# Two float32r products with exactly split activations, and query-major attention, in a two-layer hybrid block

## The chip, the core and the metric

The kernel runs on one core of a Trainium2 chip. The metric is the device time of one execution in microseconds. TensorE multiplies matrices into PSUM, VectorE and ScalarE do arithmetic and copies, GpSimd a little, SyncE issues transfers.

## The reference

The input is 8 images of 32 x 32 positions with 384 channels, all in float32. A first layer adds to each image a windowless attention with 6 heads of 64 over all 1024 positions; a second layer adds a causal attention with one head of 384 and, on the first five images, a feed-forward part whose weights are only signs:

```python
# layer 0
qkv = group_norm(x) @ qkv_w + qkv_b
attn = (q * SCALE) @ k.T + rel_h[..., None] + rel_w[..., None, :]   # per head, 1024 x 1024
x = x + softmax(attn) @ v @ proj_w + proj_b
# layer 1
t = t + softmax(causal(q @ k.T * 384**-0.5)) @ v                    # q, k, v of layer_norm(t)
h = quantize(layer_norm(t) @ sign(W1 - mean).T + b1)                # 384 -> 1536
t = t + quantize(gelu(h) @ sign(W2 - mean).T + b2)                  # 1536 -> 384
```

`quantize` scales by the largest absolute value over the whole image and clips. With 8 images and five groups, one image is a group; images 5 to 7 keep zeros here, so nothing is added to them.

## The kernel before, in words

Images follow one another. `run` loads an image as 8 tiles of 128 positions (`xt`), passes it through `layer0`, `attention1` and, for the first five, `ffn`, and stores it. A scheduler orders the instructions of each engine's queue by the data and the buffers that they need, so that pieces of neighbouring stages are mixed; within an engine they run in that order. Buffers come from pools with a fixed number of them: PSUM has two score tiles of two banks (`s_tile`) and four single banks (`o_tile`).

- `group_norm_T` (L222) reads the image a second time, already transposed by the host (`img_T`), takes statistics on VectorE, joins channels to groups and back with small matmuls (L238, L246), and scales in place (L264).
- `layer0` (L341) makes q and k (`project_T`, L295) and v (`project`, L305), and adds the relative positions as 64 further rows of q and k: small products (L379, L380), copied out by VectorE (L383) and then by ScalarE (L386).
- `attend0_fast` (L392) is key-major. For a pair of heads and a tile of 128 keys `scores` puts keys on partitions and all 1024 queries along the free dimension (L400), ScalarE takes the exp without a maximum (L404), VectorE adds the tiles of probabilities up (L412), and L416 multiplies them with v, 64 columns of weights for each head, so that two heads share the array. The probabilities are never transposed. `divide` (L421) gets the denominators by a product with ones (L428), transposes, inverts and multiplies them in. The output product (L463) follows for the 8 tiles.
- `attend1_fast` (L520) does the same for the causal attention (L531, mask L536, exp L539, values L545); a column of ones in v yields the denominator.
- `check` and `judge` gather sums and reciprocals; if one is out of bounds, a second copy of the whole program with the maximum subtracted (`attend0_general`, `attend1_general`) runs after the first. On the given inputs it does not run.
- `layer_norm_T` (L269) normalizes a tile (L284), transposes it by TensorE (L219) and copies it out (L220).
- `ffn` (L607): 12 tiles of 128 features with `w1b` (L295), bias (L614), absolute maximum (L615); after the last one the scale; then clamp (L618) and gelu (L619) over each feature tile with all 1024 positions; then for each of 8 token tiles 12 products with `w2b` (L625), bias and maximum (L626, L627), quantization and sum (L630, L631). All products are float32.
- `binarize` (L188) makes the signs at the start, in the layout of `z - (z - sign)`, five passes over a weight.

Of the kernel before, what the change touches and what calls it, by code (L numbers as in the profile page):

```python
# [9 lines left out]
F32 = mybir.dt.float32  # L10
I32 = mybir.dt.int32
# [23 lines left out]
SUM_MAX, RSUM_MAX = 1e28, 1e22  # L35


class Pools:
    def __init__(self, ctx, tc, path):
        self.path, self.fast = path, path == "f"  # L40

        def pool(name, bufs, **kw):
            return ctx.enter_context(tc.tile_pool(name=f"{path}_{name}", bufs=bufs, **kw))

        self.x = pool("x", 1)
        self.wide_ = pool("wide", 2)
        self.big_ = pool("big", 2)
        self.v_ = pool("v", 1)
        self.page_ = pool("page", 10 if self.fast else 8)
        self.work = pool("work", 2)  # L50
        self.small = pool("small", 4)
        self.ps_s = pool("ps_s", 2, space=PSUM)
        self.ps_o = pool("ps_o", 4, space=PSUM)

    def s_tile(self, name):
        return self.ps_s.tile([P, 2, 512], F32, tag="s", name=f"{self.path}_{name}")

    def o_tile(self, name):
        return self.ps_o.tile([P, 512], F32, tag="o", name=f"{self.path}_{name}")

    def big(self, name):
        return self.big_.tile([P, 2, 3, T], F32, tag="big", name=f"{self.path}_{name}")

    def wide(self, name, dtype=F32):
        return self.wide_.tile([P, NC, T], dtype, tag="wide", name=f"{self.path}_{name}")

    def page(self, name, dtype=F32):
        return self.page_.tile([P, T], dtype, tag="page", name=f"{self.path}_{name}")

    def v(self, name):  # L70
        return self.v_.tile([P, NJ, C + 1], F32, tag="v", name=f"{self.path}_{name}")


@with_exitstack
def conv_attn_hybrid(
# [3 lines left out]
    img_T: bass.AP,  # L79
# [17 lines left out]
    const = ctx.enter_context(tc.tile_pool(name="const", bufs=1))  # L97

    def load_x(pools, b):
        t = pools.x.tile([P, NJ, C], F32, tag="x", name=f"{pools.path}_x_{b}")
        src = x[b].rearrange("(j p) c -> p j c", p=P)
        for q in range(4):
            nc.sync.dma_start(out=t[:, 2 * q : 2 * q + 2, :], in_=src[:, 2 * q : 2 * q + 2, :])
        return t

# [10 lines left out]
    for half in range(2):  # L118
# [3 lines left out]
    w1b = load("w1b", [P, NC, FF], w1T.rearrange("(k p) o -> p k o", p=P), nc.scalar)  # L122
    w2b = load("w2b", [P, NM, C], w2T.rearrange("(k p) o -> p k o", p=P), nc.scalar)
# [11 lines left out]

    maskT = const.tile([P, P], F32, name="maskT")
    nc.gpsimd.memset(maskT, 0.0)
    nc.gpsimd.affine_select(
        out=maskT, in_=maskT, compare_op=ALU.is_ge, fill=MASKED, base=0, pattern=[[1, P]], channel_multiplier=-1
    )  # L140
# [30 lines left out]
    N_SEEN = B * (NPAIR + 1)  # L171
    seen = const.tile([P, 2, N_SEEN], F32, name="seen")
    flag = const.tile([1, 1], I32, name="flag")

    def judge(pools):

        bad = const.tile([P, 2, N_SEEN], F32, name="bad")
        for i, most in enumerate((SUM_MAX, RSUM_MAX)):
            nc.vector.tensor_scalar(bad[:, i, :], seen[:, i, :], most, -1.0, ALU.is_lt, ALU.mult)
        worst = const.tile([P, 1], F32, name="worst")  # L180
        nc.vector.tensor_reduce(worst, bad, AX.XY, ALU.max)
        nc.vector.tensor_scalar_add(worst, worst, 1.0)
        ps = pools.o_tile("bad")
        nc.tensor.matmul(ps[0:1, 0:1], worst, ones[:, 0:1], start=True, stop=True)
        nc.vector.tensor_copy(flag, ps[0:1, 0:1])


    def binarize(pools, w, nk, n_out, name):  # L188
        gs = n_out // NG
        n = NG * gs  # L190
        part = const.tile([P, NG], F32, name=f"part_{name}")
        for g in range(NG):
            nc.vector.tensor_reduce(part[:, g : g + 1], w[:, :, ts(g, gs)], AX.XY, ALU.add)
        tot = pools.o_tile(f"tot_{name}")
# [3 lines left out]
        z = pools.big(f"z_{name}").rearrange("p a b t -> p (a b t)")[:, : nk * n_out].rearrange("p (k o) -> p k o", k=nk)  # L198
        s = pools.big(f"s_{name}").rearrange("p a b t -> p (a b t)")[:, : nk * n_out].rearrange("p (k o) -> p k o", k=nk)
        for g in range(NG):  # L200
            nc.vector.tensor_scalar(z[:, :, ts(g, gs)], w[:, :, ts(g, gs)], mean[:, g : g + 1], None, ALU.subtract)
        z, s = z[:, :, :n], s[:, :, :n]
        nc.vector.tensor_scalar(s, z, 0.0, None, ALU.is_gt)

        nc.vector.scalar_tensor_tensor(s, z, 0.0, s, ALU.is_lt, ALU.subtract)
        nc.vector.tensor_tensor(s, s, z, ALU.add)
        nc.vector.tensor_tensor(w[:, :, :n], z, s, ALU.subtract)
        if n < n_out:
            nc.vector.memset(w[:, :, n:], 0.0)


    def stages(pools):

        def transpose_tiles(dst, srcs, engine):

            n = len(srcs)
            pt = pools.o_tile("pt")
            for i, s in enumerate(srcs):
                nc.tensor.transpose(pt[:, ts(i, P)], s, ident)  # L219
            engine(dst, pt[:, : n * P].rearrange("p (i q) -> p i q", i=n))  # L220

        def group_norm_T(b):  # L222

            xT = pools.wide(f"gnT_{b}")
            src = img_T[b].rearrange("(k p) t -> p k t", p=P)
            for k in range(NC):
                nc.sync.dma_start(out=xT[:, k, :], in_=src[:, k, :])
            st = pools.small.tile([P, NC, 2, 6], F32, tag="gst", name=f"gst_{b}")
            mv = pools.small.tile([P, NC, 2], F32, tag="gmv", name=f"gmv_{b}")
            for k in range(NC):  # L230
                for half in range(2):
                    nc.vector.bn_stats(st[:, k, half, :], xT[:, k, ts(half, 512)])
                nc.vector.bn_aggr(mv[:, k, :], st[:, k, :, :].rearrange("p a s -> p (a s)"))

            def over_groups(src, name):
                ps = pools.o_tile(name)
                for k in range(NC):
                    nc.tensor.matmul(  # L238
                        ps[:GROUPS_GN, 0:1], to_group[:, k, :], src(k), start=(k == 0), stop=(k == NC - 1)
                    )  # L240
                return ps[:GROUPS_GN, 0:1]

            def to_channels(src, n, name):
                ps = pools.o_tile(name)
                for k in range(NC):
                    nc.tensor.matmul(ps[:, k * n : (k + 1) * n], of_group[:, ts(k, P)], src, start=True, stop=True)  # L246
                return ps[:, : NC * n].rearrange("p (k n) -> p k n", k=NC)

            gm = pools.small.tile([GROUPS_GN, 2], F32, tag="gm", name=f"gm_{b}")
# [13 lines left out]
            for k in range(NC):  # L263
                nc.vector.tensor_scalar(  # L264
                    xT[:, k, :], xT[:, k, :], cs[:, k, 0:1], cs[:, k, 1:2], ALU.subtract, ALU.mult
                )
# [427 lines left out]
```

## Time and profile before

| | us |
|---|---|
| median of 3 runs | 3450.17 (3449.17 to 3451.05) |
| the profiled execution | 3451.05 |
| its span | 3449.1 |
| TensorE busy | 3191.1 |
| VectorE busy | 1345.3 |
| ScalarE busy | 851.4 |

A page of the profile gives, for each engine, the time in which it is busy; the chain of work that ended last, followed back from the end; and groups of instructions with count, busy time, mean duration in ns, and the idle time of the engine before them with what ended it. PE is TensorE's matmul, PEld its load of weights, DVE VectorE, ACT ScalarE, POOL GpSimd.[...] `f_` stands before the names of the path without a maximum.

### The profile page before, as it was taken

Reading aid. Unit: us, or ns where it says so; the run is one execution under the profiler, and the core shown is the slowest. Engines: PE = TensorE matmul, PEld = TensorE weight load, DVE = VectorE, ACT = ScalarE, POOL = GpSimd, SP = SyncE. Lnnn points to the kernel's source line nnn. Section 1 sums busy time; section 2 is a strip of 40 time slices with the busy share of each in tenths; the row PEclk is TensorE's granted clock in tenths of the full one; section 3 lists DMA queues with packets and bytes.
Section 4 is the critical chain, followed back from the end, with each engine's and each line's share of the span. In section 5 each row is a group of like instructions: output and inputs, shape, how many; then the busy total and the mean of one; then the engine's idle time right before and its main releaser. Section 6 shows DMA issues by size and latency. Waiting matters only on the chain.

```text
span 3449.1 us, 26310 instructions
## 1 busy us (share of the span) xinstructions
PE 3191.1 (93%) x10958; PEld 1525.6 (44%) x10958; DVE 1345.3 (39%) x2085; ACT 851.4 (25%) x935; POOL 163.8 (5%) x139
## 2 busy tenths in 40 slices
PE   0999998999989999989999889999899999999999
PEld 0534544435445345444354543454443454355344
DVE  7344333452233442334533344523335324523442
ACT  0332120431213321304311223213043114212320
POOL 1100002000010000020000010000200020002000
PEclk9999998999999999989999989999899999999999
DMA  4000001000000000010000010000100010000000
GB/s 147 1 0 0 0 19 37 1 0 1 0 23 32 1 0 0 19 37 1 0 0 0 19 37 0 1 0 19 37 1 0 19 37 1 0 28 28 1 0 20
DMA packets 28031, 49.03 MB, mean 14 GB/s; under 512 B 4224, under 2 KB 24064, under 8 KB 27904
## 3 DMA queue, kind: packets, MB, share of 16 engines
q1 hardware_dynamic: 20864, 37.75, 3.1%
q10 hardware_dynamic: 7040, 9.51, 0.8%
q8 instruction: 88, 1.44, 0.2%
q14 instruction: 39, 0.32, 0.0%
HBM read 34.68 MB, written 12.58 MB: 14 GB/s over the span
## 4 chain that ended last, share of the span: by engine, by line
PE 89%; DVE 6%; ACT 3%; DMA 1%; issue 0%; POOL 0%
PE f_s L400 20%; PE f_av L416 10%; PE f_y L625 9%; PE f_y L295 9%; PE f_qk L295 8%; PE f_v L305 7%; PE f_av L545 5%; PE f_s L531 5%; PE f_q L295 4%; PE f_k L295 4%; PE f_pj L305 3%; ACT f_qa L386 3%; PE f_pt L219 1%; PE f_den L428 1%; DVE f_x L631 1%; DVE f_y L630 1%
## 5 line engine op out<-in xcount | busy, mean ns | idle before, releaser
L400 PE MATMUL f_s<-f_qa,f_ka 128*128 128x512 f32 x1536 | 708.6, 607 | 8.5 <-ACT f_qa L386 8.5
L404 ACT ACTIVATE f_pr<-f_s 128x1024 f32<-128x1024 f32 x384 | 393.6, 1025 | 653.5 <-PE f_s L400 653.4
L412 DVE TENSOR_TENSOR f_sum<-f_sum,f_pr 128x1024 f32<-128x1024 f32 x288 | 351.4, 1225 | 370.2 <-ACT f_pr L404 370.2
L400 PEld LDWEIGHTS f_s<-f_qa,f_ka 128*128 128x128 f32 x1536 | 279.9, 191 | 431.0 <-issue 315.6
L416 PE MATMUL f_av<-f_pr,f_v 128*64 128x512 f32 x1536 | 366.7, 603 | 0.0
L625 PE MATMUL f_y<-w2b,f_h 128*128 128x384 f32 x960 | 325.7, 504 | 29.2 <-ACT f_h L619 29.2
L295 PE MATMUL f_y<-f_lnT,w1b 128*128 128x512 f32 x720 | 314.8, 597 | 2.8 <-ACT f_lnT L220 2.8
L295 PE MATMUL f_qk<-f_gnT,wqkv_sb 128*128 128x512 f32 x576 | 269.6, 632 | 9.5 <-DVE f_gnT L264 9.5
L625 PEld LDWEIGHTS f_y<-w2b,f_h 128*128 128x128 f32 x960 | 188.8, 197 | 167.1 <-ACT f_h L619 39.1
L295 PEld LDWEIGHTS f_y<-f_lnT,w1b 128*128 128x128 f32 x720 | 136.6, 192 | 169.4 <-issue 165.0
L416 PEld LDWEIGHTS f_av<-f_pr,f_v 128*64 128x64 f32 x1536 | 94.2, 136 | 253.6 <-issue 222.7
L545 PE MATMUL f_av<-f_v,f_pr 128*128 128x385 f32 x576 | 194.5, 486 | 0.0
L531 PE MATMUL f_s<-f_qk 128*128 128x512 f32 (+3 forms) x576 | 193.8, 486 | 0.0
L295 PEld LDWEIGHTS f_qk<-f_gnT,wqkv_sb 128*128 128x128 f32 x576 | 116.7, 204 | 156.5 <-issue 152.7
L615 DVE TENSOR_REDUCE am<-f_h 128x1 f32<-128x1024 f32 x60 | 73.2, 1220 | 248.4 <-ACT f_h L614 248.4
L545 PEld LDWEIGHTS f_av<-f_v,f_pr 128*128 128x128 f32 x576 | 108.6, 190 | 78.6 <-issue 11.5
L531 PEld LDWEIGHTS f_s<-f_qk 128*128 128x128 f32 x576 | 103.0, 190 | 83.0 <-issue 57.4
L305 PE MATMUL f_pj<-wproj_sb,f_oT 128*128 128x384 f32 x384 | 128.1, 490 | 9.6 <-DVE f_oT L439 9.6
L386 ACT COPY f_qa<-f_rel 32x384 f32<-32x384 f32 x128 | 103.0, 805 | 123.5 <-DVE f_qa L383 120.6
L354 POOL COPY f_ka<-ident 32x1024 f32<-32x1024 f32 x96 | 102.8, 1071 | 594.9 <-PE f_y L625 320.8
L295 PE MATMUL f_q<-f_lnT,wq_sb 128*128 128x512 f32 x288 | 130.3, 597 | 0.0
L295 PE MATMUL f_k<-f_lnT,wk_sb 128*128 128x512 f32 x288 | 128.8, 592 | 0.0
(125 smaller groups left out, 2519.2 us busy)
## 6 DMA issues: line engine op xcount, KB each, us to landing
f_x<-in_x SPq DMA_DIRECT2D x32, 384.0 KB, 5.1
f_gnT<-in_xT SPq DMA_DIRECT2D x24, 512.0 KB, 4.5
out_y<-f_x SPq DMA_DIRECT2D x32, 384.0 KB, 2.5
w1b<-in_w1T ACTq DMA_DIRECT2D x1, 2304.0 KB, 10.4
w2b<-in_w2T ACTq DMA_DIRECT2D x1, 2304.0 KB, 16.3
wqkv_sb<-in_qkv_w ACTq DMA_DIRECT2D x1, 1728.0 KB, 8.7
wproj_sb<-in_proj_w ACTq DMA_DIRECT2D x1, 576.0 KB, 4.5
wq_sb<-in_wq ACTq DMA_DIRECT2D x1, 576.0 KB, 17.3
```

Source lines behind the costliest of these rows:

```text
L295: nc.tensor.matmul(ps[:, half, :], w[:, k, cols], xT[:, k, ts(half, 512)], start=(k == 0), stop=(k == NC - 1),)
L305: nc.tensor.matmul(ps[:, :C], xT[:, k, ts(j, P)], w[:, k, cols], start=(k == 0), stop=(k == NC - 1))
L354: nc.gpsimd.tensor_copy(ka[r, par, p, :].rearrange("i (h w) -> i h w", h=H), unit)
L386: nc.scalar.copy(qa[rw, par, :, :].rearrange("k p (h w) -> k p w h", h=H)[:, :, 4 * g : 4 * g + 4, :], pv[rw])
L400: nc.tensor.matmul(sc[:, half, :], ka[:, par, p, ts(c, P)], qa[:, par, p, ts(half, 512)], start=True, stop=True)
L404: nc.scalar.activation(pr, sc.rearrange("p a n -> p (a n)"), AF.Exp)
L412: nc.vector.tensor_tensor(sums[par], prev, prs[par], ALU.add)
L416: nc.tensor.matmul(avs[half][ts(par, HD), :], v[:, c, ts(h, HD)], prs[par][:, ts(half, 512)], start=(c == 0), stop=(c == NJ - 1),)
L531: nc.tensor.matmul(sc[:, half, lo:], qk[:, 1, k, ts(c, P)], qk[:, 0, k, half * 512 + lo : (half + 1) * 512], start=(k == 0), stop=(k == NC ...
L545: nc.tensor.matmul(av[:, : C + 1], prs[c][:, ts(j - c, P)], v[:, c, :], start=(c == 0), stop=(c == j))
L615: nc.vector.tensor_reduce(am[:, m : m + 1], h[m], AX.X, ALU.max, apply_absolute_value=True)
L625: nc.tensor.matmul(ps[:, :C], h[m][:, ts(j, P)], w2b[:, m, :], start=(m == 0), stop=(m == NM - 1))
```

## The change

The whole attention code goes back to one form, query-major with a maximum, and the products with the sign weights change their type.

- Both attentions: scores have 128 queries on partitions and the keys along the free dimension. VectorE takes the row maximum (L303), ScalarE the exp with it as bias and the row sum as a second result (L305). Each tile of probabilities is transposed by TensorE in pieces of 128 x 128 (L188, four to a PSUM bank), copied out by VectorE and ScalarE in turn (L189), and then multiplied with v (L390, 64 columns of v per head; L438 for the causal attention). The output product follows each query tile (L403). `check`, `judge`, the second copy and the denominators by ones are gone.
- `group_norm_T` transposes the image by TensorE from `xt`; `img_T` is gone, and `xt` has two buffers.
- PSUM: `o_tile` has two banks and a new `t_tile`, for transposes and relative positions, two.
- `layer_norm_T(split=True)`: ScalarE rounds the transposed tile to float32r, VectorE stores the difference, so that high and low part add up to the value. Both are multiplied with the same signs, in float32r, into one PSUM tile. The second product does the same to gelu's result; here clamp and gelu go by token tile and half of the features, with gelu taken twice, once rounded and once full.
- `binarize` loads the weight into a working buffer and writes the signs alone, in float32r, in fewer passes.

```diff
+        pr = prob.tile([P, T], F32, tag="pr", name=f"pr_{name}")
+        nc.vector.tensor_reduce(nmax, sc[:, :n], AX.X, ALU.max, negate=True)
+        nc.scalar.activation(pr[:, :n], sc[:, :n], AF.Exp, bias=nmax, accum_out=total)
...
+            prT = transpose_probs(pr, NJ, f"prT0_{b}_{j}_{h}")
+            for c in range(NJ):
+                nc.tensor.matmul(av[:, ts(h, HD)], prT[:, c, :], v[:, c, ts(h, HD)], start=(c == 0), stop=(c == NJ - 1))
...
+        pipelined([(j, h) for j in range(NJ) for h in range(NH)], scores, values)
...
+            def hi_lo(dst, ps):
+                nc.scalar.copy(dst, ps)
+                nc.vector.tensor_tensor(xlo[:, :, ts(j, P)], ps, dst.bitcast(F32), ALU.subtract)
...
-                ps = project_T(w1b, ts(m, P), xT, f"y1_{b}_{m}")
+            n = NC * len(xs)
+            for i in range(n):
+                for half in range(2):
+                    nc.tensor.matmul(
+                        ps[:, half, :], w1s[:, i // 2, ts(m, P)], xs[i % 2][:, i // 2, ts(half, 512)],
+                        start=(i == 0), stop=(i == n - 1),
+                    )
...
-            for m in range(NM):
-                nc.vector.tensor_scalar(h[m], h[m], up, low, ALU.min, ALU.max)
-                nc.scalar.activation(h[m], h[m], AF.Gelu, scale=s)
+        def activate(j, half):
+            part = halves[half][:, :, ts(j, P)]
+            nc.vector.tensor_scalar(part, part, up, low, ALU.min, ALU.max)
...
+            nc.scalar.activation(hi, part, AF.Gelu, scale=s)
+            nc.scalar.activation(part, part, AF.Gelu, scale=s)
+            nc.vector.tensor_tensor(lo, part, hi.bitcast(F32), ALU.subtract)
+            return hi, lo
...
-                    nc.tensor.matmul(ps[:, :C], h[m][:, ts(j, P)], w2b[:, m, :], start=(m == 0), stop=(m == NM - 1))
+                for m in range(6):
+                    for i in range(2):
+                        nc.tensor.matmul(
+                            ps[:, :C], hs[i][:, m, :], w2s[:, half * 6 + m, :],
+                            start=(half == m == i == 0), stop=(half == i == 1 and m == 5),
+                        )
...
-            xT = pools.wide(f"gnT_{b}")
-            src = img_T[b].rearrange("(k p) t -> p k t", p=P)
+                transpose_tiles(
+                    xT[:, k, ts(half, 512)].rearrange("p (i q) -> p i q", i=4),
+                    [xt[:, half * 4 + i, ts(k, P)] for i in range(4)],
+                    nc.scalar.copy,
+                )
```

## The prediction

> **What bounds the kernel now.** I read the page's shares first, then its chain and costliest groups.
>
> ```profile
> span 3449.1 us, 26310 instructions
> PE 3191.1 (93%) x10958; PEld 1525.6 (44%) x10958; DVE 1345.3 (39%) x2085; ACT 851.4 (25%) x935; POOL 163.8 (5%) x139
> ...
> PE 89%; DVE 6%; ACT 3%; DMA 1%; issue 0%; POOL 0%
> ...
> L400 PE MATMUL f_s<-f_qa,f_ka 128*128 128x512 f32 x1536 | 708.6, 607 | 8.5 <-ACT f_qa L386 8.5
> ...
> L416 PE MATMUL f_av<-f_pr,f_v 128*64 128x512 f32 x1536 | 366.7, 603 | 0.0
> L625 PE MATMUL f_y<-w2b,f_h 128*128 128x384 f32 x960 | 325.7, 504 | 29.2 <-ACT f_h L619 29.2
> L295 PE MATMUL f_y<-f_lnT,w1b 128*128 128x512 f32 x720 | 314.8, 597 | 2.8 <-ACT f_lnT L220 2.8
> ```
>
> TensorE is busy for 93% of the span and is 89% of the chain; almost no idle time stands before these groups. So the time is TensorE's sum, plus its few gaps. The program issues 768 score products and the row counts 1536: a float32 product is two records.
>
> The second image, cut into stages by the window view (first row: its qkv products; then relative positions, first attention with its output product, norm and q, k, v of the second attention, second attention, norm and w1, w2, and the gap to the next image):
>
> ```profile
> 563.00:612.00 49.00, 48.93 (x122) 23.71 (x124) 12.94 (x15) 6.66 (x6) 6.68 (x1) 0.95 0.10 33
> 612.00:626.60 14.60, 13.54 (x257) 12.02 (x257) 9.36 (x17) 12.19 (x16) 0.00 (x0) 1.00 0.01 2
> 626.60:780.30 153.70, 152.50 (x456) 56.97 (x456) 75.02 (x90) 52.46 (x51) 0.11 (x1) 1.00 0.00 0
> 780.30:834.40 54.10, 51.41 (x146) 26.43 (x146) 13.01 (x23) 6.98 (x12) 0.00 (x0) 0.97 0.00 1
> 834.40:881.00 46.60, 46.55 (x144) 25.99 (x143) 14.35 (x45) 7.77 (x10) 0.00 (x0) 1.00 0.00 1
> 881.00:951.80 70.80, 66.87 (x168) 30.75 (x168) 19.19 (x28) 16.12 (x20) 0.00 (x0) 0.98 0.00 0
> 951.80:1022.80 71.00, 65.16 (x195) 37.83 (x195) 22.43 (x42) 16.26 (x15) 3.93 (x5) 0.95 0.06 23
> 1022.80:1040.90 18.10, 3.04 (x25) 2.69 (x24) 14.95 (x33) 0.20 (x1) 9.62 (x10) 0.56 0.23 87
> ```
>
> (Columns: stretch, length, busy us and count of PE, PEld, DVE, ACT, POOL, then clock, DMA share, GB/s.) Five images take 477.9 us like this one; three without feed-forward about 324. VectorE and ScalarE work half the first attention or less: there is room beside TensorE, not on it.
>
> Prices of TensorE, from the timeline of the first image and the view of two tiles:
>
> ```profile
> 253.35 1.94 PE L416 MATMUL f_av<-f_pr,f_v 128*64 128x512 f32 x8
> ...
> 255.22 3.70 PE L400 MATMUL f_s<-f_qa,f_ka 128*128 128x512 f32 x8
> ```
>
> ```profile
> 309.67 0.82 PE L219 MATMUL f_pt<-ident,xn 128*128 128x128 f32 x6
> ```
>
> ```profile
> L246 PE MATMUL f_cmean<-gm,of_group x48: 245/245/347, 60.9 to 3117.8; 32*128 32x1 f32 x48
> ```
>
> The values of two heads begin at 253.35 and the scores behind them at 255.22, so they take 1.87; the next values begin at 258.85, so eight score records take 3.63: 0.43 us each where one follows the other, and 0.2 for the changes between the two kinds. Six transposes end after 0.82 us, one lasts 0.273: (0.82-0.273)/5 = 0.109 us from start to start. The six records of the group mean of channels last 0.82 with one at 0.245: 0.115, though each streams one column. Both load 128 columns of weights.
>
> **What the Trainium skill says.** "TensorE: Matmul & The Clock Gate", section "LDWEIGHTS (loading the stationary operand)": a load takes its columns divided by 1.2 ns, so 107 ns for 128, whatever the rows. The 0.109 and 0.115 agree: a short stream is hidden below its load. "FP8 and Floating Point Precision", section "TensorE Precision Notes": full float32 is four passes, reduced float32 is read truncated. The trace agrees for the full one: 2 x 0.43 = 0.86 us for 512 columns is four times 512 columns at 2.4 GHz. No row shows float32r. "ScalarE: Activation LUTs", section "What ACT_TABLE_LOAD costs": a bias by pointer adds 93 ns; L614 with one takes 1114, L404 without 1025, so 89.
>
> **First attention.** Per image 48 turns (head, query tile). A turn before: scores 1.82, values 0.94, sums of L428 0.12 = 2.88; 48 of them and the output product's 15.5 give 153.7, the stage as seen. After: scores 4 x 0.43 = 1.72; 8 transposes of probabilities at 0.109 = 0.87; 8 value products of 64 columns with 128-column weights, each two records at 0.112 (load-bound; streaming alone would be 0.053) = 1.79. Together 4.38, 210.2 an image. The output product stays (48 records of 0.322) and 24 transposes of its input come (2.6). Waits: VectorE gets a maximum (1.22, as L615) and a copy of four transposed tiles (0.69, as L439), ScalarE an exp (1.11) and a copy (0.59, L220's 0.48 plus 128 columns). That is 1.91 and 1.70 under 4.38; the additions of L412 (1.225) go. The order of the built program puts a half of the next scores (0.86) between transposes and values: the first copy is ready some 0.3 + 0.69 us after its four transposes, and TensorE reaches its reader after 0.44 + 0.86. Behind a waiting value product stand the rest of the scores and the next turn's transposes, and for these both copying engines wait. Only when a maximum is just running on VectorE is the copy later; I take 0.15 a turn, 0.5 at each of 8 query tiles where the division stands, 2.6 for the emptying at the end: 14. Sum 242.3 for 153.7: **+88.6 an image, +709**.
>
> **Second attention.** 36 transposes more, 3.9, and waits at the ends, where a row of scores must pass mask, maximum and exp before its transposes: I take 3. The 385th column goes. **+7 an image, +56.**
>
> **Relative positions.** Their PSUM tile now comes from a pool of two, not four. One tile lives 0.67 (matmuls) + 0.17 + 0.56 (L383) + 0.81 (L386, which waits for L383) + handovers 0.1 = 2.3; two tiles give 1.15 a group for today's 14.6/16 = 0.91. 16 x 0.26 = 4.2: **+34**.
>
> **Feed-forward, five images.** One float32r pass is unknown here: from below one pass, 0.216 for 512 columns (a quarter of 0.86); from above the full price. I take one pass, because the four passes that the trace shows are what a split into parts costs. w1: 144 x 0.216 = 31.1 for 144 x 0.43 = 61.9 records: -30.8. The norm before it also makes the low parts on VectorE: 0.48 + 0.56 for each of 8 tiles instead of about 0.5: +4. w2: 192 products of 384 columns, 0.162 each, 31.1 for 62. But now they start on two feeds. VectorE needs 16 clamps (0.68, from L618's 0.81), 16 subtractions (0.96), 8 times bias and maximum (1.11), and two statistics: 36.6; ScalarE 16 x 2 gelus of 0.92: 29.5. The order puts eight clamps before the first subtraction, so the second product waits 3.9 + 8 x 0.68 + 0.96 = 10.3 us after w1's end, where 5.84 was. Then VectorE's pace sets the end: 44 us for 71.0: -27. Sum **-53.8, x5 = -269**. If float32r cost as much as float32, +31 on w1 and +27 on w2 an image came back: +290.
>
> **Between images.** Group norm makes its own transpose: 24 at 0.109 and 6 copies on ScalarE lie under w2; but four of six statistics (0.67) now stand behind w2's last tile on VectorE, and its whole chain behind the quantization, which cost 12 us of gap before: +3.5 x5, +4 x3 for the others, +1.5 x8 for the norm after the first attention: **+42**. The load of the next input has two buffers and stays hidden. At the start two of five long passes of each binarization go (4 x 4.9), but w2's load now waits for w1's buffer (about 7 us for 2.3 MB) and transposes and statistics enter: **-8**. The judging at the end (below 2) goes.
>
> **Sum.** +709 +56 +34 -269 +42 -8 = +564. Against the profiled execution of 3451.05 (span 3449.1; median of the runs 3450.17, the same within 0.03%): 4015. The waits in attention are my softest term and I lean a little below: **4000 us**.
>
> **Rivals.** *Waits take over in attention.* Transposes, copy and values are one chain through three in-order queues; were each copy late by a maximum (1.22), a turn would be 5.3: +0.77 x 384 = +295, **4295**. For it: one copy and one maximum share VectorE each turn; against: the order's cover of 0.86. *float32r is no faster:* **4290**. *No waits at all:* a turn of 4.38, nothing at the tiles' ends: -110 to -150, **3870**. *Faster:* if short products and transposes ran at their streaming time (0.053 a record, weight loads 128 columns wide hidden or shared), a turn would be 1.72 + 0.43 + 0.85 = 3.0, +8 to +11 an image, and the feed-forward gain would carry: 3451 - 269 + 124 + 80 = **3386**. It decides from a turn below about 3.2 us (145 us spare over 384 turns). The 0.109 and 0.115 speak against it. *The change doing nothing* is excluded: both paths are rewritten for all images.
>
> **How the numbers follow.** Forecast 0.60 (its own range 3890 to 4120), waits 0.15, float32r no faster 0.10, no waits 0.11, faster 0.03, something within 0.2% (about what a measurement of this kernel can tell) 0.01. The range from 3840 to 4260 takes in forecast, no waits and the milder half of the waits. Slower 0.96, same 0.01, faster 0.03.
>
> **What would show it.** Right: value records of the first attention 0.112 us apart; transposes at 0.109; that stage 235 to 250 us an image; w1 records 0.216 apart; w2 stage about 44 with VectorE before it; TensorE still above 85% busy. Wrong: TensorE idle before the values by copies for more than 0.5 us a turn; float32r records at 0.43; or 64-column records well under 0.1.

## The result, and the profile after

| | median | range | runs |
|---|---|---|---|
| before | 3450.61 us | 3449.17 to 3451.73 | 4 |
| after | 3994.98 us | 3989.35 to 3996.12 | 4 |

The ratio is 1.1575 (95% interval 1.1555 to 1.1595): the change makes the kernel 544 us slower. The prediction was 4000, in a range from 3840 to 4260. The profiled execution of after has a span of 3992.4 us, 543.3 more than before's 3449.1.

The page of after, its shares, its chain and the groups that answer to those shown of before:

```profile
span 3992.4 us, 44746 instructions
...
PE 3635.8 (91%) x19116; PEld 2530.5 (63%) x19116; DVE 1725.2 (43%) x2608; ACT 1290.8 (32%) x2012; POOL 167.6 (4%) x129
...
PE 87%; DVE 7%; ACT 2%; POOL 1%; issue 1%; DMA 1%; ACTq 0%; POOLq 0%; DVEq 0%
...
L376 PE MATMUL s<-ka,qa 128*128 128x512 f32 x1536 | 782.4, 611 | 12.6 <-ACT pr L305 6.8
...
L390 PE MATMUL av<-v,prT 128*128 128x64 f32 x6144 | 739.7, 271 | 2.8 <-DVE prT L189 2.8
...
L188 PE MATMUL pt<-ident,pr 128*128 128x128 f32 x3360 | 463.8, 273 | 9.5 <-ACT prT L189 9.5
...
L502 PE MATMUL y<-sign_w,hi 128*128 128x384 f32 x480 | 169.4, 353 | 32.2 <-ACT hi L489 32.2
...
L356 PE MATMUL rel<-qa,rel 64*32 64x96 f32 x1024 | 141.6, 343 | 36.6 <-ACT qa L363 36.6
```

TensorE is still the bound, at 91% of the span and 87% of the chain; it has 8,158 records more. (A record is one entry of the profile; it lasts longer than the distance to the next: the score records last 611 ns on average, and where they follow each other they start 0.43 us apart.) The value products of the first attention (L390) were 1536 records of 512 columns and 366.7 us; they are 6144 records of 64 columns and 739.7 us. The transposes (L188) are new. The idle times that count stand before the relative positions (36.6) and before w2 (32.2). Before all 1536 score records of the eight images it is 12.6, before all value records 2.8: the first attention itself hardly waits. In 200 us of its middle, in the second image, TensorE has no gap at all:

```profile
700.00:900.00 200.00, 200.00 (x1251) 152.50 (x1250) 93.33 (x121) 78.07 (x136) 0.00 (x0) 1.00 0.00 1
```

The second image again, by the stages of before that differ (columns as there: stretch, length, busy us and count of PE, PEld, DVE, ACT, POOL, then clock, DMA share, GB/s):

```profile
658.10:682.00 23.90, 18.58 (x258) 15.48 (x257) 9.36 (x17) 12.06 (x16) 0.00 (x0) 0.58 0.00 1
682.00:915.10 233.10, 230.06 (x1416) 173.59 (x1416) 104.22 (x133) 90.58 (x155) 0.00 (x0) 0.99 0.00 1
...
968.80:1022.00 53.20, 51.79 (x181) 29.53 (x179) 23.33 (x54) 9.64 (x21) 0.00 (x0) 1.00 0.00 1
1022.00:1066.40 44.40, 39.34 (x176) 31.34 (x176) 22.86 (x32) 16.70 (x21) 0.00 (x0) 0.96 0.00 1
1066.40:1114.20 47.80, 39.03 (x210) 38.08 (x210) 36.50 (x61) 33.42 (x39) 7.69 (x8) 0.89 0.00 1
1114.20:1137.80 23.60, 3.91 (x23) 3.46 (x22) 16.11 (x35) 2.16 (x4) 13.55 (x8) 0.54 0.38 134
```

Stage by stage, after less before, beside the prediction's term:

| stage of an image | before | after | difference | predicted |
|---|---|---|---|---|
| relative positions | 14.6 | 23.9 | +9.3 | +4.2 |
| first attention, output product | 153.7 | 233.1 | +79.4 | +88.6 |
| second attention | 46.6 | 53.2 | +6.6 | +7 |
| norm and w1 | 70.8 | 44.4 | -26.4 | -26.8 |
| w2 | 71.0 | 47.8 | -23.2 | -27 |
| gap to the next image | 18.1 | 23.6 | +5.5 | +3.5 |

The first qk product starts at 81.6 us for 84.0 (-2.4; predicted -8). Eight times the first three and five times w1 and w2 give 762 - 248 = +514; with the start the sum is +512, and the remaining 31 us lie between the images and in the norms (predicted +42).

### The profile page after: what moved, and what is told of

It reads as the page before. It is cut to its first block, busy times and chain, and to the rows that moved or that the text cites. A ratio compares the mean times of both kernels' runs of the same rounds, so it can differ in the third digit from the quotient of the medians.

```text
span 3992.4 us, 44746 instructions
## 1 busy us (share of the span) xinstructions
PE 3635.8 (91%) x19116; PEld 2530.5 (63%) x19116; DVE 1725.2 (43%) x2608; ACT 1290.8 (32%) x2012; POOL 167.6 (4%) x129
## 2 busy tenths in 40 slices
DMA packets 24647, 37.54 MB, mean 9 GB/s; under 512 B 3840, under 2 KB 23680, under 8 KB 24448
## 4 chain that ended last, share of the span: by engine, by line
PE 87%; DVE 7%; ACT 2%; POOL 1%; issue 1%; DMA 1%; ACTq 0%; POOLq 0%; DVEq 0%
PE s L376 17%; PE av L390 17%; PE pt L188 11%; PE qk L276 7%; PE v L286 6%; PE av L438 5%; PE s L424 5%; PE y L473 4%; PE y L502 3%; PE pj L286 3%; PE k L276 3%; PE q L276 3%; PE rel L356 2%; ACT qa L363 1%; POOL ka L331 1%; DVE qa L360 1%
## 5 line engine op out<-in xcount | busy, mean ns | idle before, releaser
L390 PEld LDWEIGHTS av<-v,prT 128*128 128x128 f32 x6144 | 751.1, 192 | 174.0 <-DVE prT L189 101.6
L376 PE MATMUL s<-ka,qa 128*128 128x512 f32 x1536 | 782.4, 611 | 12.6 <-ACT pr L305 6.8
L303 DVE TENSOR_REDUCE nmax<-s 128x1 f32<-128x1024 f32 (+1 forms) x448 | 516.9, 1154 | 614.3 <-PE s L376 603.0
L390 PE MATMUL av<-v,prT 128*128 128x64 f32 x6144 | 739.7, 271 | 2.8 <-DVE prT L189 2.8
L305 ACT ACTIVATE pr<-s,nmax 128x1024 f32<-128x1024 f32 (+1 forms) x448 | 476.4, 1063 | 614.8 <-DVE nmax L303 614.8
L189 ACT COPY prT<-pt 128x512 f32<-128x512 f32 (+3 forms) x416 | 238.3, 573 | 827.5 <-PE pt L188 820.6
L188 PE MATMUL pt<-ident,pr 128*128 128x128 f32 x3360 | 463.8, 273 | 9.5 <-ACT prT L189 9.5
L188 PEld LDWEIGHTS pt<-ident,pr 128*128 128x128 f32 x3360 | 393.8, 146 | 107.7 <-issue 81.9
L189 DVE COPY prT<-pt 128x512 f32<-128x512 f32 (+1 forms) x448 | 300.5, 672 | 199.6 <-PE pt L188 192.7
L276 PE MATMUL qk<-gnT,wqkv_sb 128*128 128x512 f32 x576 | 268.1, 629 | 8.9 <-DVE gnT L235 8.9
L438 PE MATMUL av<-v,prT 128*128 128x384 f32 x576 | 200.0, 492 | 7.3 <-DVE prT L189 7.3
L502 PE MATMUL y<-sign_w,hi 128*128 128x384 f32 x480 | 169.4, 353 | 32.2 <-ACT hi L489 32.2
L356 PE MATMUL rel<-qa,rel 64*32 64x96 f32 x1024 | 141.6, 343 | 36.6 <-ACT qa L363 36.6
L438 PEld LDWEIGHTS av<-v,prT 128*128 128x128 f32 x576 | 105.4, 190 | 93.8 <-DVE prT L189 34.1
L357 PE MATMUL rel<-qa,rel 64*32 64x96 f32 x1024 | 148.4, 343 | 0.0
```

The source lines that it names most:

```text
L276: nc.tensor.matmul(ps[:, half, :], w[:, k, cols], xT[:, k, ts(half, 512)], start=(k == 0), stop=(k == NC - 1),)
L303: nc.vector.tensor_reduce(nmax, sc[:, :n], AX.X, ALU.max, negate=True)
L305: nc.scalar.activation(pr[:, :n], sc[:, :n], AF.Exp, bias=nmax, accum_out=total)
L356: nc.tensor.matmul(ps[r0 : r0 + 32, ts(i, 96)], rel[src, 0, win], qv[:, :, at, :], start=True, stop=True)
L376: nc.tensor.matmul(sc[:, half, :], qa[:, par, p, ts(j, P)], ka[:, par, p, ts(half, 512)], start=True, stop=True)
L390: nc.tensor.matmul(av[:, ts(h, HD)], prT[:, c, :], v[:, c, ts(h, HD)], start=(c == 0), stop=(c == NJ - 1))
```

## The experiments

Each kernel was timed beside the kernel before on the same chip (3447 to 3452 us throughout); ratios are to it. After stands at 3995.

| kernel | what differs | median us | ratio (95% interval) |
|---|---|---|---|
| v_wide | after, value products of 128 columns | 4016.23 | 1.1644 (1.1624 to 1.1663) |
| v_half | after, value products of 32 columns | 4040.65 | 1.1716 (1.1696 to 1.1735) |
| no_tr | after, no transposes of probabilities | 3686.43 | 1.0689 (1.0671 to 1.0707) |
| no_max | after, no maximum before the exp | 4039.72 | 1.1708 (1.1689 to 1.1728) |
| psum4 | after, one PSUM pool of four banks | 3953.42 | 1.1458 (1.1441 to 1.1476) |
| ffn_f32 | after, feed-forward in float32 | 4239.10 | 1.2291 (1.2272 to 1.2310) |
| no_pb | after, no addition of the bias pb | 3968.95 | 1.1508 (1.1493 to 1.1524) |
| no_clamp | after, no clamps before the gelu | 3987.46 | 1.1560 (1.1541 to 1.1580) |
| bef_f32r | before, with the changed feed-forward | 3176.38 | 0.9209 (0.9195 to 0.9223) |
| bef_f32r_gn | the same, group norm moved ahead | 3158.53 | 0.9156 (0.9141 to 0.9172) |
| bef_f32r_gn_bin | the same, sign weights made later | 3145.99 | 0.9121 (0.9106 to 0.9136) |
| bef_f32r_gn_bin2 | the same, their sums on GpSimd | 3112.62 | 0.9022 (0.9007 to 0.9037) |

### Are the short value products bound by their weights?

The largest term of the prediction was 16 value records a turn at 0.112 us, the price of loading 128 weight columns, where 64 columns of streaming alone would be 0.053. Two kernels change only the number of moving columns.

```diff
-                nc.tensor.matmul(av[:, ts(h, HD)], prT[:, c, :], v[:, c, ts(h, HD)], start=(c == 0), stop=(c == NJ - 1))
+                nc.tensor.matmul(av[:, ts(p2, P)], prT[:, c, :], v[:, c, ts(p2, P)], start=(c == 0), stop=(c == NJ - 1))
```

(p2 = h // 2.)

> The changed kernel with value products of 128 columns (the head's pair) in place of 64; even and odd head of a pair write the same 128 columns, so the output is another one and the multiplications of this group double. Load theory (a record costs the 0.109-0.112 us of its 128 weight columns, and 64 or 128 moving columns are hidden below it): 3995 to 4015, records still 0.112 apart. Streaming theory (a record costs something fixed and 0.054 us for 64 columns on top): 6144 x 0.054 = +330, about 4325, records 0.165 apart.

```diff
-                nc.tensor.matmul(av[:, ts(h, HD)], prT[:, c, :], v[:, c, ts(h, HD)], start=(c == 0), stop=(c == NJ - 1))
+                nc.tensor.matmul(av[:, ts(h, HD // 2)], prT[:, c, :], v[:, c, ts(h, HD // 2)], start=(c == 0), stop=(c == NJ - 1))
...
-                o.rearrange("p (h d) -> p h d", h=NH), av[:, :C].rearrange("p (h d) -> p h d", h=NH),
+                o.rearrange("p (h d) -> p h d", h=NH),
+                av[:, : HD].unsqueeze(1).to_broadcast([P, NH, HD]),
```

> The changed kernel with value products of 32 columns in place of 64; the other half of each head is left out (the division reads the first 64 columns for every head). Load theory: 3995, records still 0.112 apart, although half of the product is left out. Streaming theory: 6144 x 0.027 = -165, about 3830, records 0.085 apart.

4016 and 4041: v_wide is 1 us above the range of the load theory, v_half outside both of its expectations. The timeline of TensorE shows the records themselves (columns: start us, length us, engine, line, operation, tiles, shapes, count); a run of sixteen, and the group that begins next, of after:

```profile
701.48 1.89 PE L390 MATMUL av<-v,prT 128*128 128x64 f32 x16
703.22 1.04 PE L188 MATMUL pt<-ident,pr 128*128 128x128 f32 x8
```

of v_half:

```profile
1240.92 1.87 PE L390 MATMUL av<-v,prT 128*128 128x32 f32 x16
1242.63 1.10 PE L376 MATMUL s<-ka,qa 128*128 128x512 f32 x2
```

and of v_wide:

```profile
1240.01 1.95 PE L391 MATMUL av<-v,prT 128*128 128x128 f32 x16
1241.79 1.02 PE L376 MATMUL s<-ka,qa 128*128 128x512 f32 x2
```

From the first record to the next group it is 1.71 us for 32 columns, 1.74 for 64 and 1.78 for 128, which is 0.107, 0.109 and 0.111 a record. Four times the columns cost 4%. That is the price stated for a load in the Trainium skill, "TensorE: Matmul & The Clock Gate", section "LDWEIGHTS (loading the stationary operand)": columns of weights divided by 1.2 ns, 107 ns for 128. The streaming theory asked for -165 and +330 us and is out. After's turn holds 8 products of 64 columns, and the same time would hold 8 of 128. Of the 2.4 us that v_wide's first attention is longer in an image, the records explain 1.9 (768 x 0.0025).

v_half does no more work than after and is 46 us slower. Its first attention is 6 us an image longer, although TensorE is idle in it for no longer than in after (3 us in both). The windows of its end, in the third image, show why:

```profile
1440.00:1448.00 8.00, 6.92 (x55) 5.97 (x55) 2.80 (x4) 2.28 (x4) 0.00 (x0) 1.00 0.01 2
1448.00:1456.30 8.30, 7.14 (x33) 6.28 (x32) 1.25 (x2) 1.05 (x2) 0.00 (x0) 0.51 0.00 0
1456.30:1460.00 3.70, 3.64 (x6) 1.83 (x6) 0.00 (x0) 1.29 (x2) 0.00 (x0) 0.50 0.00 0
```

For the last 12 us TensorE ran at a clock of 0.5: half of that, 6 us, is what it lost. At the same place in after (905 to 912.8 us, second image) the clock is 1.00. The scheduler had put the instructions of TensorE's queue into another order for the other sizes, and with it the end of the stage. The Trainium skill, same page, section "What's actually happening", says that TensorE's clock is halved or full according to how busy it has been lately; this trace shows the two values, 0.50 and 1.00, but not what tips it: TensorE was busy for 6.92 of the 8 us before it fell, and for 6.33 of 7.8 us in after, where it did not fall.

### Are the transposes paid in full?

```diff
-            prT = transpose_probs(pr, NJ, f"prT0_{b}_{j}_{h}")
+            prT = pr.rearrange("p (j q) -> p j q", j=NJ)
```

> The changed kernel with the transposes of the first attention's probabilities and their copies left out; the value products take the untransposed tile as weights. If TensorE's sum alone sets the turn: 3072 transposes x 0.109 = -335, plus the turn's waits of 5 us an image, -40: 3620 to 3660. If the turn is set by the chain of copies and maxima beside TensorE (waits theory), more than 400 us go: below 3595. If ScalarE or VectorE set the turn already, less than 250 go.

3686.43, so 309 us less: between the ranges that were expected, 26 us above the nearest. The stage, in the third image:

```profile
1132.40:1325.00 192.60, 189.12 (x1032) 133.94 (x1032) 75.18 (x88) 64.93 (x107) 0.00 (x0) 0.99 0.00 1
```

It is 192.6 us for 233.1: -40.5 an image, -324 in all, against 48 x 8 x 0.109 x 8 = 335 for the transposes alone. TensorE's idle time in it (192.6 - 189.1 = 3.5 us, for 3.0) did not go with them, so it was not a wait for the transposes' copies, and the 40 us that were to go on top stayed. Some 15 us came back elsewhere, most of it between the second attention's start and w1 (1.5 us an image). So the transposes' own time was gained almost whole, and no wait with it: TensorE's sum sets the turn.

### Does the maximum hold anything up?

```diff
-        nmax = small.tile([P, 1], F32, tag="nmax", name=f"nmax_{name}")
-        nc.vector.tensor_reduce(nmax, sc[:, :n], AX.X, ALU.max, negate=True)
...
-        nc.scalar.activation(pr[:, :n], sc[:, :n], AF.Exp, bias=nmax, accum_out=total)
+        nc.scalar.activation(pr[:, :n], sc[:, :n], AF.Exp, accum_out=total)
```

> The changed kernel without the maximum before the exp, in both attentions (the exp is taken of the score itself). If the maximum lies wholly beside TensorE in the first attention: its 5 us of waits an image and 3 us in the second attention are the most that can go, 3930 to 3995. If the copies that wait behind a maximum on VectorE set the turn (1.22 us for each of 384): 3525 to 3700.

4039.72, 45 us more than after, outside both expectations. The 392 maxima over 1024 columns are 478 us of VectorE in after, and nothing of that was gained. So the rival in which copies wait behind maxima is out. The loss has two parts. The built order differs, and up to the first product behind it the stage is 5.6 us an image longer; in the third image the last 13 us of it:

```profile
1450.00:1463.00 13.00, 9.73 (x49) 6.66 (x49) 2.72 (x6) 2.72 (x5) 0.00 (x0) 0.74 0.00 0
```

The clock was 1.00 in the 10 us ahead of them; 0.74 over 13 us costs 3.4 us. That is not all, but the rest is no waiting: within the stage (237.6 us for 233.1) TensorE is idle for 2.4 us, in after for 3.0. With the half clock at both ends taken off (4.5 us, in after 2.0), the same 1416 records take some 2.6 us more in their new order.

A difference of 40 us between two kernels of this family thus says nothing about the part that was edited until the clock at the stage's end has been looked at.

### What makes the relative positions 9.3 us longer?

```diff
-    ps_t = pool("ps_t", 2, space=PSUM)
-    ps_o = pool("ps_o", 2, space=PSUM)
+    ps_o = pool("ps_o", 4, space=PSUM)
...
-        return ps_t.tile([P, 512], F32, tag="t", name=name)
+        return ps_o.tile([P, 512], F32, tag="o", name=name)
```

> The changed kernel with its two PSUM pools of two banks (t and o) made into one of four; the computation is the same. If the pool of two holds up the relative positions: that stage goes from 23.9 us back to about 14.6, 8 x 9.3 = -74, about 3920. If the copies' own order on VectorE and ScalarE is the cause, the stage stays at 23.9 and the time at 3995, give or take the 45 us that a new order of the first attention was worth in the last two runs.

The stage went back to 14.7 us in every image, as expected; the whole time lies above the 3920 expected with it. In after, from its start, and in psum4, in the window view:

```profile
658.00:662.00 4.00, 3.21 (x50) 2.51 (x52) 1.66 (x3) 1.60 (x2) 0.00 (x0) 1.00 0.00 0
662.00:670.00 8.00, 6.08 (x86) 5.00 (x82) 3.30 (x6) 4.03 (x6) 0.00 (x0) 0.51 0.01 2
670.00:682.00 12.00, 9.39 (x129) 8.00 (x129) 4.40 (x8) 6.43 (x9) 0.00 (x0) 0.50 0.00 1
```

```profile
664.00:678.80 14.80, 13.75 (x258) 12.15 (x257) 9.37 (x17) 12.23 (x16) 0.00 (x0) 1.00 0.01 2
```

With two banks TensorE waits, its clock falls to half after 4 us, its matmuls take twice as long, and a bank lives longer still; the same 258 records are 13.75 us busy in psum4 and 18.58 in after. With four banks the clock stays at 1.00. The whole is only 42 us faster, not 74: the transposes of the first input now share their pool with the sums of the sign weights and come behind them, so the first product starts at 93.0 us for 81.6. The norm and the q, k and v products before the second attention take 1.1 us more in the second image (54.8 us at a clock of 0.93, for 53.7 at 0.97), the second attention 0.7, and w1 2 us in the five images that have it: some 24 us in all.

### What is each half of the change worth?

ffn_f32 takes the float32r products out of after:

```diff
-        sign = const.tile([P, nk, n_out], F32R, name=f"sign_{name}")
+        sign = const.tile([P, nk, n_out], F32, name=f"sign_{name}")
...
-        xs = layer_norm_T(xt, f"2_{b}", split=True)
+        xs = layer_norm_T(xt, f"2_{b}")
...
+            ps = project_T(w1s, ts(m, P), xs, f"y1_{b}_{m}")
...
-            nc.scalar.activation(hi, part, AF.Gelu, scale=s)
             nc.scalar.activation(part, part, AF.Gelu, scale=s)
-            nc.vector.tensor_tensor(lo, part, hi.bitcast(F32), ALU.subtract)
-            return hi, lo
+            return [part]
```

> The changed kernel with its feed-forward in float32 (one product, no split), gelu still by token tile and half; the attentions stay as changed. If float32r is what saves: norm and w1 go from 44.4 back to about 70.8, w2 from 47.8 to 62-71 (62 is its sum of float32 records), 5 x (26.4 + 14 to 23) = +202 to +247, 4197 to 4242. If w2's gain came from the gelu by token tile, w2 stays near 48 and only w1's 132 come back: about 4127.

bef_f32r puts after's split norm, its binarizing, its two loops of products and its gelu by token tile into the kernel before, with the split tiles in its page pool and the second transposed norm in its wide pool:

```diff
-                for m in range(NM):
-                    nc.tensor.matmul(ps[:, :C], h[m][:, ts(j, P)], w2b[:, m, :], start=(m == 0), stop=(m == NM - 1))
+                for half in range(2):
+                    hs = activate(j, half)
+                    for m in range(6):
+                        for i in range(2):
+                            nc.tensor.matmul(
+                                ps[:, :C], hs[i][:, m, :], w2b[:, half * 6 + m, :],
+                                start=(half == m == i == 0), stop=(half == i == 1 and m == 5),
+                            )
```

> The kernel before with the changed feed-forward alone (split norm, float32r signs, gelu by token tile and half); its attentions stay key-major. If the two halves of the change are independent: norm and w1 -26.4, w2 -23 to -31 (five pairs of split tiles instead of three), gap and start as before: 5 x -(49 to 57) = -247 to -287, 3163 to 3203. If the second wide tile of the split norm and the split tiles hold up the next image's input and the gap grows by 5 us each: up to 3230.

ffn_f32 is 4239.10 and bef_f32r is 3176.38, both inside what float32r and independence expect. The feed-forward saves 244 us on top of the changed attentions and 273 on the old ones; what remains of the change without it, the attentions above all, costs 790 us. The window over w2, from the end of w1 to the last product, is back at its old length in ffn_f32 although the gelu is still by token tile, and 44.8 us in bef_f32r:

```profile
1143.00:1214.60 71.60, 64.79 (x200) 38.29 (x200) 21.47 (x42) 16.59 (x21) 4.69 (x6) 0.95 0.00 1
```

```profile
871.80:916.60 44.80, 36.56 (x194) 35.69 (x194) 36.35 (x62) 32.63 (x35) 5.53 (x6) 0.89 0.10 36
```

So w2's gain is float32r's, not the loop order's.

### What sets w2's start and its pace?

```diff
             part = halves[half][:, :, ts(j, P)]
-            nc.vector.tensor_scalar(part, part, up, low, ALU.min, ALU.max)
```

> The changed kernel without the 16 clamps to +-127 before the gelus of each image (they are left out; only the largest element would differ, in its last places). If the clamps queued ahead of the first subtraction hold up w2's second product, and VectorE's sum sets its pace: the wait before it falls from some 10 us to 5 or 6 after w1's end and 16 x 0.60 = 9.5 us go from VectorE's row, w2 stage from 47.8 to 37-41, 5 x 7 to 11 = -35 to -55: 3940 to 3960. If w2's pace is set by ScalarE and the number of split tiles, only the start moves: 5 x 4 = -20, about 3975. If by TensorE's sum, nothing moves: 3995.

3987.46: 8 us gone where 35 to 55 were expected, 20 under the second theory and nothing under the third, TensorE's sum, to which it is nearest. The timeline of after, from the scale to the second product (rows of PEld left out):

```profile
1070.04 4.81 DVE L484 TENSOR_SCALAR h<-h,qu,ql 128x768 f32<-128x768 f32 x8
1070.79 1.28 ACT L489 ACT_TABLE_LOAD   x1 [3.82 <-DVE h L484]
1072.09 1.76 ACT L489 ACTIVATE hi<-h,qs 128x768 fp32r<-128x768 f32 x2
...
1073.08 0.69 PE L502 MATMUL y<-sign_w,hi 128*128 128x384 f32 x1 [6.71 <-ACT hi L489]
1073.76 1.75 ACT L490 ACTIVATE h<-h,qs 128x768 f32<-128x768 f32 x2
1074.76 1.83 DVE L491 TENSOR_TENSOR lo<-h,hi 128x768 fp32r<-128x768 f32 x2
...
1075.77 0.69 PE L502 MATMUL y<-sign_w,lo 128*128 128x384 f32 x1 [2.01 <-DVE lo L491]
```

and of no_clamp:

```profile
1070.01 1.28 ACT L488 ACT_TABLE_LOAD   x1 [3.04 <-DVE ql L460]
...
1073.92 1.83 DVE L490 TENSOR_TENSOR lo<-h,hi 128x768 fp32r<-128x768 f32 x2 [3.93 <-ACT h L489]
...
1074.94 0.69 PE L501 MATMUL y<-sign_w,lo 128*128 128x384 f32 x1 [1.96 <-DVE lo L490]
```

The eight clamps end at 1074.85, just when the first subtraction can start in any case: ScalarE must load its table and run two gelus for the high parts and one for the full value before it. Without clamps the second product comes 0.83 us earlier. After that, after's w2 window shows TensorE busy without a break:

```profile
1076.00:1114.20 38.20, 38.11 (x209) 37.56 (x209) 28.59 (x45) 27.65 (x33) 7.31 (x7) 0.92 0.00 1
```

VectorE is busy for 28.59 of 38.2 us there. TensorE sets the pace.

### Which operation is stopped between the images?

The trace of after had shown a VectorE operation on three elements a partition that lasts 4.18 us, exactly as long as GpSimd's addition of pb still runs:

```profile
1125.57 7.44 POOL L320 TENSOR_TENSOR x<-x,pb 128x3072 f32<-128x3072 f32 x1 [7.00 <-DMA out_y<-x]
...
1128.66 0.16 DVE L225 TENSOR_TENSOR gd<-gmv,cmean 128x3 f32<-128x3 f32 x1 [1.53 <-PE cmean L217]
1128.85 4.18 DVE L226 TENSOR_TENSOR gd<-gd 128x3 f32<-128x3 f32 x1
...
1132.97 2.11 POOL L331 COPY ka<-ident 32x1024 f32<-32x1024 f32 x2
1133.07 0.95 DVE L227 TENSOR_TENSOR gd<-gd,gmv 128x3 f32<-128x3 f32 x1
```

```diff
-        nc.gpsimd.tensor_tensor(xt, xt, pb.unsqueeze(1).to_broadcast([P, NJ, C]), ALU.add)
```

> The changed kernel without GpSimd's addition of the output product's bias to x (7.3 us for each image; the bias is left out). If that addition blocks the small VectorE operation on the group statistics that runs during it (4178 ns median, 988 before): this one falls to 1000 ns or less and each passage to the next image is 3 to 5 us shorter, 3960 to 3975. If the operation is slow for another reason, it stays at 4178 and the time at 3992 to 3998.

3968.95, as the first expectation has it. In the view of the tile gd (min/median/max ns), after and then no_pb:

```profile
L226 DVE TENSOR_TENSOR gd<-gd x8: 154/4178/4193, 72.5 to 3568.8; 128x3 f32<-128x3 f32 x8
L227 DVE TENSOR_TENSOR gd<-gd,gmv x8: 155/949/950, 77.5 to 3572.3; 128x3 f32<-128x3 f32 x8
```

```profile
L226 DVE TENSOR_TENSOR gd<-gd x8: 154/161/163, 72.6 to 3547.0; 128x3 f32<-128x3 f32 x8
L227 DVE TENSOR_TENSOR gd<-gd,gmv x8: 154/161/161, 77.6 to 3547.2; 128x3 f32<-128x3 f32 x8
```

Each passage to a next image is 3.5 to 3.8 us shorter. The Trainium skill, "SBUF — State Buffer", section "Who interferes with whom", says that a VectorE instruction with two SBUF inputs contends with a GpSimd instruction that reads SBUF, over ports that only one of them can hold at a time. The trace agrees: L226 and L227 have two such inputs and last until the end of a GpSimd instruction, L226 of the addition and L227 of the first of the two copies behind it; L225, with one input from PSUM, takes 0.16 us in the middle of it.

### A kernel faster than both

bef_f32r is already 273 us faster than before. Three further edits go into its order.

The group norm of the next image is called ahead of the quantization that ends the feed-forward:

```diff
+                quantize = ffn(xt, b) if b < B_FFN else None
+                if b + 1 < B:
+                    xT = group_norm_T(b + 1)
+                if quantize:
+                    quantize()
```

> The kernel before with the changed feed-forward, and the group norm of the next image put ahead of the quantization that ends the feed-forward (its statistics need only the next input). If the passage of 18.0 us is the group norm's scaling standing behind the quantization's 16 operations on VectorE: it falls to 10 to 12, 5 x 6 to 8 = -30 to -40, 3136 to 3146. If the group norm's own chain through TensorE and ScalarE sets it, less than 10 us go in all: 3166 to 3176.

3158.53, between the two expectations. The passage falls from 18.0 to 11.4 us, as the first has it, 33 us over five; but in four images qkv goes from 48.0 to 49.6 us and the first attention from 159.1 to 160.7, 13 us in all, and the start is 1.2 later. The clock accounts for most of these 3.2 us an image: in the third image it is 0.50 over the first 5.6 us of qkv (0.75 over the first 5.7 in bef_f32r), and 0.76 over the first 6 us of the first attention (1.00 there).

Then the sign weights are made group by group after the first image's first attention, instead of all of them ahead of everything:

```diff
-        binarize(pools, w1T, w1b, NC, FF, "w1")
-        binarize(pools, w2T, w2b, NM, C, "w2")
...
+                if b == 0 and pools.fast:
+                    binarize(pools, w1T, w1b, NC, FF, "w1")
+                    binarize(pools, w2T, w2b, NM, C, "w2")
```

> As the last kernel, and the sign weights are made group by group between the first and the second attention of the first image, in place of all of them ahead of the first group norm (the computation is the same). If the 82 us before the first product are VectorE's binarizing and the loads it waits for: they fall to about 30, 50 us go, and some 30 us of VectorE's work (10 groups of about 3 us) lie beside the second attention of the first image, of which up to 20 may show: 3108 to 3130. If the first input and the group norm's chain set the start themselves, nothing goes and the 20 to 30 us come on top: 3175 to 3190.

3145.99, outside both expectations: the first product starts at 30.1 us for 82.8, as the first has it, but the first image's passage from its first to its second attention grows by 38 us, where up to 20 were allowed for. The timeline of TensorE names the cause:

```profile
252.73 0.59 PE L201 MATMUL f_tot_w<-part_w,ones 128*128 128x1 f32 x2 [5.60 <-DVE part_w L199]
```

Ten products of one column stand at the head of TensorE's queue, nine of them wait for VectorE (5.6 us and eight times 3.8), and the norm's transposes stand behind them.

```diff
-            nc.tensor.matmul(tot[:, :1], ones, part, start=True, stop=True)
+            nc.gpsimd.partition_all_reduce(tot, part, P, bass_isa.ReduceOp.add)
```

> As the last kernel, with the ten sums over partitions of the sign weights' means taken by GpSimd in place of ten one-column products. In the last kernel these stand in TensorE's queue ahead of the second attention's norm, and TensorE stood still for 5.6 + 8 x 3.8 = 36 us before them. If that queue is the whole of it: -30 to -39, 3107 to 3116. If the norm then waits as long for VectorE, which makes the signs: 3140 to 3146.

3112.62, 33 us less, as expected of the queue. This is 337 us below before and 882 below after.

## Why the prediction was right, point by point

**The first attention** was the sum's main part, and its records were priced rightly: turns of 4.38 us from records of 0.43, 0.109 and 0.112. v_half and v_wide show that the value records are bound by their weights, no_tr that the transposes are paid almost in full. The stage is 233.1 us, where 242.3 were forecast; without any wait the working had 210.2 + 15.5 + 2.6 = 228.3. The waits of 14 were mis-sized by more than a factor of four. TensorE is idle for 3.0 us of the stage (233.10 - 230.06), at its two ends; the assumed 0.15 a turn and 0.5 a tile do not occur, as the 200 us without a gap show. Another 2.0 us are not a wait but the half clock over the stage's first 4.4 us (0.55), which the working did not have. So 233.1 also lies just below the 235 to 250 that were to show that the prediction is right.

**The second attention**, +6.6 for +7, and **norm and w1**, -26.4 for -26.8, came as worked out. The records of the float32r products, in w1 and in w2 (16 of them from the first of these lines to the second, 18 from the third to the fourth):

```profile
1040.02 0.62 PE L473 MATMUL y<-lnT,sign_w 128*128 128x512 f32 x2
...
1043.68 0.62 PE L473 MATMUL y<-lnT,sign_w 128*128 128x512 f32 x2
...
1084.79 0.33 PE L502 MATMUL y<-sign_w,hi 128*128 128x384 f32 x1
...
1087.91 0.33 PE L502 MATMUL y<-sign_w,hi 128*128 128x384 f32 x1
```

In w1 they are 0.229 us apart, not 0.216, which is 1.9 us over 144 records; the norm beside them was a little shorter than assumed. A float32 product of 512 columns takes 0.86 us, 3.8 times as long as such a record, so the assumption of one pass for four was nearly right. (The 2.4 GHz that the prediction sets beside the four passes is a figure of the Trainium skill, "TensorE: Matmul & The Clock Gate", section "What's actually happening"; the traces here show only shares of the clock.)

**Relative positions**: the mechanism (two banks instead of four) is shown by psum4. The size was off, +9.3 for +4.2: the working put 0.67 us of matmuls into a bank's life at the clock of before. With the waits the clock fell to 0.5, and these matmuls took twice as long: 2.3 + 0.67 is 2.97 for a bank, 1.49 for a group with two banks, and 16 groups make the 23.8 that the trace shows as 23.9. The working also has a slip: 1.15 less 0.91 is 0.24, and 16 of them are 3.8, not 4.2.

**w2** came near its number for a partly wrong reason. "The order puts eight clamps before the first subtraction" holds, and so do the 10.3 us before the second product (10.0 from the end of w1's last product, at 1065.8), but the clamps are not what it waits for; ScalarE's table load and gelus take as long. "VectorE's pace sets the end" failed: TensorE does. From the second product to the end of the last, at 1112.0, it takes 36.2 us: the records are 0.173 apart, not 0.162, and 17 of the first, at the half clock, 0.32. Behind them stand 16 of the next input's transposes, 2.2 us. With the 9.4 before the second product (from 1066.4, where the window begins) this makes 47.8, for the forecast's 44.

**Between the images** +42 was forecast and +31 is left. That the group norm's chain stands behind the quantization was seen; that GpSimd's addition stops it for 4 us was not. Where no feed-forward stands between two images, the time from the last product of the one to the first qkv product of the other went from 5.0 to 14.4 us, +9.4 for the forecast's +4 (there are two such places, not three); that the norm after the first attention gave -0.4 (53.7 us for 54.1) and not +1.5 made up for it. The **start** gave -2.4, not -8: the group norm's last steps stand behind the second binarizing in VectorE's queue.

The errors are 8 x -9.2 = -74 in the first attention, +41 in relative positions, +21 in the feed-forward, -11 between images, +6 at the start and -3 in the second attention. They sum to -20, and the sum of 4015 became 3995. So the 4000 owe part of their closeness to luck, to errors of both signs. Of the rivals, "waits take over" is excluded by no_max, no_tr and the 200 us without a gap, "float32r is no faster" by ffn_f32, and "streaming time" by v_half and v_wide.

## What to carry to other kernels

With a stationary operand of 128 columns, this kernel's float32 products cost the same for 32, 64 or 128 moving columns, so put the long dimension on the moving side: the key-major form moves 512 columns for each load and needs no transposes, which is worth 635 us in the first attention here. A change with two halves should be priced and tried by halves: the feed-forward alone gains 273 us. Where an experiment that removes work comes out slower, look first at the granted clock at the ends of the stages, and at what a new order put at the head of TensorE's queue.

## What the runs showed of the hardware that was not expected

- The granted clock goes from 1.00 to 0.50 within a stage in which TensorE is busy for four fifths of the time (3.21 of 4.0 us in the relative positions of after), and stays there into the dense work behind it: over the first six score records, from 682.0 to 686.4 us, it is still 0.55. What tips it is open. In the second image of after the stretches at 0.50 last 3.4, 10.2, 23.9 and 27.3 us, which is 1, 3, 7 and 8 times 3.41.
- A float32r record costs 0.229 us for 512 columns and 0.173 for 384 at full clock, which is 14 and 12 ns more than a quarter of what the float32 product of that length costs in two records (2 x 0.43 / 4 = 0.215 and 2 x 0.322 / 4 = 0.161).
- A VectorE operation on 3 elements took 4178 ns while GpSimd added in SBUF, and 161 ns without.
- The exp with a running sum issues a second ScalarE instruction of 196 ns to read the sum (448 of them, 87.8 us); it lies beside TensorE here.
